# Graph attention over edge lists: extra columns in half-wide products, two-bank sums, and a later reciprocal

## The chip, the core and the metric

The kernel runs on one core of one Trainium2 chip. Times are device microseconds of a whole execution; the median of several runs is compared. The engines are TensorE (PE in the profile, its weight loads PEld), VectorE (DVE), ScalarE (ACT), GpSimd (POOL) and the queue that starts plain transfers (SP). TensorE writes its products into PSUM, the accumulator memory; the other data live in SBUF, the working memory, or in the main memory (DRAM).

## What is computed

Three graph attention layers over one graph of 4096 nodes, with features of width 512. The reference, cut to its core (`k` and `h` run over heads, `n` and `m` over nodes):

```python
# layer 0: 8 heads of 64, then a residual and a layer norm
h   = einsum('nf,kfp->knp', x, W)
f1  = einsum('knp,kp->kn', h, a_src); f2 = einsum('knp,kp->kn', h, a_dst)
e   = leaky_relu(f2[:, :, None] + f1[:, None, :], 0.2)
att = softmax(where(adj > 0, e, -1e16), axis=-1)
x   = layernorm(x + concat_heads(einsum('knm,kmp->knp', att, h)))
# layer 1: 8 heads of 64 (W1, a1), elu; then one head of 512 (Wo, ao), elu; then two dense layers
x1  = elu(concat_heads(gat_heads(x, adj, W1, a1)))
out = elu(gat_heads(x1, adj, Wo, ao))
out = relu(out @ lin1_w + lin1_b) @ lin2_w + lin2_b
x   = layernorm(x + out)
```

Everything is float32. The graph is sparse (on average 8 neighbours) with degrees that fall from the first node to the last: node `i` is joined to node `j` with a probability that is proportional to `1 / sqrt((i+1)(j+1))`.

## The kernel before

Nodes are taken in 32 tiles of 128. A first stage turns each tile's rows of the adjacency into lists of edges: `idx` holds the neighbour of each edge, `nl` the node that it belongs to, in chunks of 128 edges, separately for the two halves of 64 nodes of a tile. A tile of low degree has 6 chunks, the densest has 55, and a layer has 339. Beside it, each tile of `x` is projected. (A dense version of everything stands ready for graphs that don't fit the lists; it doesn't run here.)

A layer's input is a table in DRAM with one row per node: 512 projected features and, for each head, `d`, the part of the score that depends on the neighbour. The part that depends on the node itself, `s`, stays in SBUF. Both are products of the node's features with the weights' sums `wa` (the projection weights times the attention vector):

```python
def project_in(sb, ps, st, src, t, tag="pa"):
    pt = ps.tile([P, FC, P], F32, name="pt")
    for c in range(FC):                                   # FC = 4 blocks of 128 features
        nc.tensor.transpose(pt[:, c, :], src[:, ts(c, P)], ident)
    xt = sb.tile([P, FC, P], F32, name="xt")
    for c in range(FC):
        nc.scalar.activation(xt[:, c, :], pt[:, c, :], AF.Copy, accum_out=st.xparts[:, c, t : t + 1])
    ph = ps.tile([P, hs, dm], F32, name="ph")             # 512 columns: the features
    for c in range(FC):
        nc.tensor.matmul(ph, xt[:, c, :], st.w[:, c], start=(c == 0), stop=(c == FC - 1))
    pa = ps.tile([P, 2, hs], F32, name="pa", tag=tag)     # 16 or 2 columns: s and d
    for c in range(FC):
        nc.tensor.matmul(pa, xt[:, c, :], st.wa[:, c], start=(c == 0), stop=(c == FC - 1))
    return ph, pa

def project_out(sb, st, ph, pa, t, n=P):
    hrow = ...
    nc.scalar.copy(hrow[:, :F], ph[:n].rearrange("p h d -> p (h d)"))
    nc.scalar.copy(hrow[:, F:], pa[:n, 1, :])
    nc.sync.dma_start(st.table[t * P : t * P + n, :], hrow)
    if t < NT:
        nc.scalar.copy(st.s[:, t, :], pa[:, 0, :])
```

A tile's chunks are worked in units of up to 6. `gather` fetches, for each chunk, the 128 neighbours' rows of the table by one indirect transfer that GpSimd issues, into one of five buffers `g`. `spread` brings `s` of a tile's nodes to its edges by small products (`pss`), summed up by VectorE (`collect`). `weights` computes the exponent of each edge and head, `add` sums:

```python
def weights(self, u):
    nc.vector.tensor_add(zz, u.pick(self.s[u.t], base), d)            # d: columns 512 and on of g
    nc.vector.scalar_tensor_tensor(z, z, ALPHA, z, op0=OP.mult, op1=OP.max)
    nc.vector.tensor_sub(zz, zz, u.pick(self.ls[u.t], base))
    u.w = self.wk.tile([P, GC, hs], F32, name="w")
    nc.scalar.activation(u.w[:, : u.n], z, AF.Exp)
    if hs > 1:
        u.wp = self.ps.tile([P, GC, hs], F32, name="wp")              # the same in PSUM
        nc.scalar.activation(u.wp[:, : u.n], z, AF.Exp)

def add(self, u):
    if u.first:
        self.acc[u.t] = self.pacc.tile([P, F], F32, name="acc")       # two buffers
        self.den[u.t] = self.pacc.tile([P, hs], F32, name="den", bufs=1)
    # sm[edge, node] is 1 where the edge belongs to the node
    ...
    sums(self.den[u.t], (lambda k: u.w[:, k]) if hs > 1 else (lambda k: ones))
    if hs > 1:
        body = u.g[:, :n, :F].rearrange("p n (h w) -> p n h w", h=hs)
        nc.vector.tensor_mul(body, body, u.wp[:, :n, :, None].to_broadcast([P, n, hs, DM]))
    sums(self.acc[u.t], lambda k: u.g[:, k, :F])
```

`sums` makes one product per chunk, `sm` being the stationary side, into the 64 partitions of its half. The loop of a heads layer, each tile's normalization, transposition, projection and row store being spread over the steps that follow:

```python
def divide(t):                                  # o = acc * rd, residual, statistics (or the elu)
    o = at.normal(sb, t)
    return norm, t, o, finish(o, t, extra.pop(t))
def norm(t, o, rest):
    rest()                                      # the end of the layer norm (or of the elu)
    return project, t, o
def project(t, o):
    return rows, t, *project_in(pp, ps, nxt, o, t)
def rows(t, ph, pa):
    project_out(pp, nxt, ph, pa, t)
    if t % 8 == 0:
        split_s(pp, nxt, t, 8)

for i, u in enumerate(units):
    ...
    if u.first and pos + 2 < NT:
        spread = at.spread(order[pos + 2])
    run(project)
    if i + 1 < len(units):
        at.weights(units[i + 1])
    at.add(u)
    if i + GB < len(units):
        at.gather(units[i + GB])
    if u.last:
        at.inverse(sb, u.t)                     # rd = 1 / den
    run(rows)
    run(norm)
    if u.first and pos > 0:
        ways.append((divide, order[pos - 1]))
        run(divide)
    if spread:
        spread()
```

The order of instructions on each engine is that of this text in the three attention stages; each engine works its own list in order. The third stage (one head of 512) has a loop of the same kind, with `inverse` at the same place and the two dense layers between its units.

Of the kernel before, what the change touches and what calls it, by code (L numbers as in the profile page):

```python
# [32 lines left out]
HC = HID // P  # L33
ALPHA = 0.2
# [498 lines left out]
def sparse_path(  # L533
# [56 lines left out]
    class Stage2:  # L590
        def __init__(self, name, heads, dim, dest_first):
            self.name, self.heads, self.dim, self.dest_first = name, heads, dim, dest_first
            self.row = F + heads
            self.table = dram.tile([N + 1, self.row], F32, name=f"table_{name}")
            self.s = const.tile([P, NT, heads], F32, name=f"ss_{name}")
            self.s3 = const.tile([P, NT, 2, 3, heads], BF16, name=f"s3_{name}")
            self.xparts = const.tile([P, FC, NT], F32, name=f"xparts_{name}")
# [7 lines left out]
    def load_projection(pool, st, w, a):  # L605

        hs, dm = st.heads, st.dim
        st.w = pool.tile([P, FC, hs, dm], F32, name=f"sw_{st.name}")
        for c in range(FC):
            nc.sync.dma_start(st.w[:, c], w[:, ts(c, P), :].rearrange("k f o -> f k o"))  # L610
        st.wa = pool.tile([P, FC, 2, hs], F32, name=f"swa_{st.name}")
        with tc.tile_pool(name=f"swload_{st.name}", bufs=2) as wp:
            for side in range(2):
                ab = wp.tile([P, hs, dm], F32, name="sab")
                nc.sync.dma_start(ab, a[:, ts(side, dm)].partition_broadcast(P))
                at = side if st.dest_first else 1 - side
                for c in range(FC):
                    prod = wp.tile([P, hs, dm], F32, name="sprod")
                    nc.gpsimd.tensor_mul(prod, st.w[:, c], ab)
                    nc.vector.tensor_reduce(st.wa[:, c, at, :], prod, AX.X, OP.add)  # L620

    def project_in(sb, ps, st, src, t, tag="pa"):

        hs, dm = st.heads, st.dim
        pt = ps.tile([P, FC, P], F32, name="pt")
# [7 lines left out]
        ph = ps.tile([P, hs, dm], F32, name="ph")  # L633
        for c in range(FC):
            nc.tensor.matmul(ph, xt[:, c, :], st.w[:, c], start=(c == 0), stop=(c == FC - 1))  # L635
        pa = ps.tile([P, 2, hs], F32, name="pa", tag=tag)
        for c in range(FC):
            nc.tensor.matmul(pa, xt[:, c, :], st.wa[:, c], start=(c == 0), stop=(c == FC - 1))  # L638
        return ph, pa

    def project_out(sb, st, ph, pa, t, n=P):

        hrow = sb.tile([P, F + HS], F32, name="hrow")[:n, : st.row]
        nc.scalar.copy(hrow[:, :F], ph[:n].rearrange("p h d -> p (h d)"))  # L644
        nc.scalar.copy(hrow[:, F:], pa[:n, 1, :])
        nc.sync.dma_start(st.table[t * P : t * P + n, :], hrow)
        if t < NT:
            nc.scalar.copy(st.s[:, t, :], pa[:, 0, :])
# [17 lines left out]
    def project_mean(sb, ps, st, tag="pa"):  # L666

        hs, dm = st.heads, st.dim
# [3 lines left out]
        ph = ps.tile([P, hs, dm], F32, name="ph")  # L672
        for c in range(FC):
            nc.tensor.matmul(ph[:1], mean[:, c : c + 1], st.w[:, c], start=(c == 0), stop=(c == FC - 1))
        pa = ps.tile([P, 2, hs], F32, name="pa", tag=tag)
        for c in range(FC):
            nc.tensor.matmul(pa[:1], mean[:, c : c + 1], st.wa[:, c], start=(c == 0), stop=(c == FC - 1))
        project_out(sb, st, ph, pa, NT, 1)
# [224 lines left out]
    class Attention:  # L903
# [64 lines left out]
        def weights(self, u):  # L968
# [3 lines left out]
            zz = z.rearrange("p (m g) h -> p m g h", g=u.hn)  # L972
            d = u.g[:, : u.n, F : self.st.row].rearrange("p (m g) h -> p m g h", g=u.hn)
            nc.vector.tensor_add(zz, u.pick(self.s[u.t], base), d)  # L974
            nc.vector.scalar_tensor_tensor(z, z, ALPHA, z, op0=OP.mult, op1=OP.max)
            nc.vector.tensor_sub(zz, zz, u.pick(self.ls[u.t], base))
            u.w = self.wk.tile([P, GC, hs], F32, name="w")
            nc.scalar.activation(u.w[:, : u.n], z, AF.Exp)  # L978
            if hs > 1:

                u.wp = self.ps.tile([P, GC, hs], F32, name="wp")
                nc.scalar.activation(u.wp[:, : u.n], z, AF.Exp)  # L982

        def add(self, u):

            hs, n = self.st.heads, u.n
            if u.first:
                self.acc[u.t] = self.pacc.tile([P, F], F32, name="acc")
                self.den[u.t] = self.pacc.tile([P, hs], F32, name="den", bufs=1)
# [25 lines left out]
            def sums(out_, rows):  # L1015
                for k, (first, stop) in enumerate(flags):
                    h = k % u.hn
                    nc.tensor.matmul(out_[h * HN : (h + 1) * HN], sm[:, k], rows(k), start=first, stop=stop)  # L1018

            sums(self.den[u.t], (lambda k: u.w[:, k]) if hs > 1 else (lambda k: ones))  # L1020
            if hs > 1:
                body = u.g[:, :n, :F].rearrange("p n (h w) -> p n h w", h=hs)
                nc.vector.tensor_mul(body, body, u.wp[:, :n, :, None].to_broadcast([P, n, hs, DM]))  # L1023
            sums(self.acc[u.t], lambda k: u.g[:, k, :F])

        def inverse(self, sb, t):
            self.den[t], den = sb.tile([P, self.st.heads], F32, name="rd"), self.den[t]
            nc.vector.reciprocal(self.den[t], den)  # L1028

        def normal(self, sb, t):  # L1030
            o = sb.tile([P, F], F32, name="o")
            acc, rd = self.acc.pop(t), self.den.pop(t)
            if self.st.heads > 1:
                nc.vector.tensor_tensor(
                    o.rearrange("p (h w) -> p h w", w=DM),
                    acc.rearrange("p (h w) -> p h w", w=DM),
                    rd[:, :, None].to_broadcast([P, HS, DM]),
# [329 lines left out]
```

## Time and profile before

| | |
|---|---|
| median of 3 runs | 2692.4 us (2692.3 to 2696.59) |
| profiled execution | 2661.6 us, mean TensorE clock granted 0.846 |
| TensorE products / weight loads busy | 1993.7 us (75%) / 873.6 us (33%) |
| VectorE busy | 1507.3 us (57%) |
| ScalarE busy | 669.1 us (25%) |
| GpSimd busy | 1096.1 us (41%) |
| first gather of the three attention stages | 690, 1280 and 1861 us |

How to read the profile: a group is one line of the kernel on one engine, with the tiles written and read, the shape and the count; after the bar come its busy time, the mean ns of one instruction, and how long the engine was idle just before such instructions and what it waited for. "issue" is idle time in which nothing that the profile shows was waited for, and "remote" a releaser that it doesn't know. Line 1018 is the product inside `sums`, 635 and 638 are the two products of `project_in`, 644, 645 and 648 the copies of `project_out`, 914 is the gather, 1023 VectorE's multiply in `add`, 1028 the reciprocal, 1034 the normalization, 940 and 949 the products and the sum of `spread`. In a table of stretches each engine has its busy us and, in brackets, its instructions; PEclk is the granted share of TensorE's full clock. In a timeline a row has the start, the duration of the merged instructions, engine, line, operation, tiles, shape and count.

### The profile page before, as it was taken

What the parts mean: (1) busy time and instruction counts of PE and PEld (TensorE: products, weight loads), DVE (VectorE), ACT (ScalarE), POOL (GpSimd) and SP (SyncE); (2) the same over time, 40 slices, a digit from 0 to 9 for tenths busy, and PEclk for the clock granted to TensorE, in tenths of its full rate; (3) what the DMA queues carried; (4) which work ended last, traced back from release to release, by engine and by line L of the source; (5) the groups of instructions that cost most, each with busy time, mean ns of one, the idle gap of its engine ahead of it and who ended that gap; (6) DMA issues with size and microseconds to landing.
All of it is one profiled execution on the core that took longest, in us unless ns stands there. A gap on an engine that the chain in (4) does not pass through costs nothing. (4 is left out here: it accounts for less than half of the span.)

```text
span 2661.6 us, 27663 instructions
## 1 busy us (share of the span) xinstructions
PE 1993.7 (75%) x8501; PEld 873.6 (33%) x8501; DVE 1507.3 (57%) x4485; ACT 669.1 (25%) x1870; POOL 1096.1 (41%) x1204
## 2 busy tenths in 40 slices
PE   1125779999468787757488777666497999999998
PEld 0002234344134333323144333322243444444433
DVE  4998777788367777755356666553223233333331
ACT  1001233444045433221133222110121223322221
POOL 6100000000455666663646666553646544444310
PEclk9556678899689988877699888778697999999999
DMA  6101345564467877763556667564546444455421
GB/s 177 40 32 48 115 150 191 206 222 150 140 187 214 238 232 229 208 194 105 161 164 180 186 182 196 163 175 154 166 141 176 144 143 149 137 144 151 139 72 37
DMA packets 138069, 415.19 MB, mean 156 GB/s; under 512 B 33515, under 2 KB 33523, under 8 KB 133814
## 3 DMA queue, kind: packets, MB, share of 16 engines
q0 software_dynamic: 81360, 269.62, 36.2%
q1 hardware_dynamic: 56550, 143.70, 15.5%
q8 instruction: 70, 1.15, 0.2%
q14 instruction: 89, 0.73, 0.1%
HBM read 371.00 MB, written 42.23 MB: 155 GB/s over the span
## 5 line engine op out<-in xcount | busy, mean ns | idle before, releaser
L914 POOL DMA_INDIRECT g<-table_t,idx x1017 | 1029.4, 1012 | 846.4 <-PE acc L1018 305.3
L1018 PE MATMUL acc<-g,sm 128*64 128x512 f32 x2034 | 611.1, 682 | 80.6 <-issue 45.8
L635 PE MATMUL ph<-sw_t,xt 128*128 128x512 f32 x768 | 426.8, 698 | 97.9 <-issue 57.3
L1023 DVE TENSOR_TENSOR g<-g,wp 128x2048 f32<-128x2048 f32 (+4 forms) x148 | 383.4, 2591 | 33.1 <-ACT wp L982 23.0
L1018 PEld LDWEIGHTS acc<-g,sm 128*64 128x64 f32 x2034 | 169.8, 152 | 314.7 <-issue 270.5
L635 PEld LDWEIGHTS ph<-sw_t,xt 128*128 128x128 f32 x768 | 157.2, 220 | 282.2 <-issue 206.2
L1028 DVE RECIPROCAL rd<-den 128x8 f32<-128x8 f32 (+1 forms) x96 | 18.7, 194 | 388.1 <-PE den L1018 158.4
L765 POOL COPY over<-lst 128x1 f32<-128x1 f32 x35 | 6.6, 189 | 553.1 <-DVE lst L760 500.4
L1262 PE MATMUL p<-sl2w,shid 128*128 128x512 f32 x512 | 229.2, 600 | 3.3 <-DVE xr L1267 2.7
L1250 PE MATMUL p<-sht,sl1w 128*128 128x512 f32 x512 | 225.5, 596 | 0.0
L745 DVE MAX8 cand<-key 128x8 f32<-128x353 f32 (+55 forms) x467 | 204.9, 448 | 24.0 <-PE key L739 23.5
L729 ACT ACTIVATE sg<-raw 128x4096 bf16<-128x4096 int32 x32 | 116.0, 3625 | 217.7 <-PE key L738 208.8
L630 ACT ACTIVATE xt<-pt 128x128 f32<-128x128 f32 x384 | 101.1, 282 | 272.9 <-PE pt L627 127.3
L738 PE MATMUL key<-sg,s_identb 128*128 128x512 bf16 (+1 forms) x258 | 115.1, 446 | 48.2 <-DVE cand L745 28.0
L1262 PEld LDWEIGHTS p<-sl2w,shid 128*128 128x128 f32 x512 | 95.1, 191 | 137.4 <-issue 119.8
L1250 PEld LDWEIGHTS p<-sht,sl1w 128*128 128x128 f32 x512 | 95.5, 190 | 129.8 <-issue 124.9
L1018 PE MATMUL den<-w,sm 128*64 128x8 f32 x1356 | 71.8, 209 | 84.7 <-issue 38.3
L974 DVE TENSOR_TENSOR z<-s,g 128x48 f32<-128x48 f32 (+6 forms) x222 | 40.9, 184 | 150.7 <-DMA g<-table_t,idx 131.5
L644 ACT COPY hrow<-ph 128x512 f32<-128x512 f32 (+1 forms) x99 | 57.9, 585 | 271.6 <-PE ph L635 193.1
L1005 DVE TENSOR_SCALAR sm<-iota_n,nl,w 128x64 f32<-128x64 f32 x339 | 83.8, 325 | 71.1 <-ACT w L978 71.1
L638 PEld LDWEIGHTS pa<-swa_t,xt 128*128 128x128 f32 x768 | 106.8, 206 | 39.6 <-issue 24.2
L739 PE MATMUL key<-frac,ones_b 64*128 64x512 bf16 (+1 forms) x258 | 115.3, 447 | 0.0
(131 smaller groups left out, 2185.1 us busy)
## 6 DMA issues: line engine op xcount, KB each, us to landing
raw<-in_adj_dram SPq DMA_DIRECT2D x32, 2048.0 KB
table_t<-hrow SPq DMA_DIRECT2D x64, 260.0 KB
xr<-in_x_dram SPq DMA_DIRECT2D x64, 256.0 KB
g<-table_t,idx POOLq DMA_INDIRECT x1017
table_t<-hrow SPq DMA_DIRECT2D x32, 256.5 KB
sx_d<-o SPq DMA_DIRECT2D x32, 256.0 KB
xr<-sx_d SPq DMA_DIRECT2D x32, 256.0 KB
out_dram<-xr SPq DMA_DIRECT2D x32, 256.0 KB
```

Of the source, the lines that this page charges most:

```text
L630: nc.scalar.activation(xt[:, c, :], pt[:, c, :], AF.Copy, accum_out=st.xparts[:, c, t : t + 1])
L635: nc.tensor.matmul(ph, xt[:, c, :], st.w[:, c], start=(c == 0), stop=(c == FC - 1))
L638: nc.tensor.matmul(pa, xt[:, c, :], st.wa[:, c], start=(c == 0), stop=(c == FC - 1))
L729: nc.scalar.activation(sg, raw, AF.Sign)
L738: nc.tensor.matmul(key[:, j - w0_ : e - w0_], ident_b, sg[:, j:e], start=True, stop=False)
L739: nc.tensor.matmul(key[:, j - w0_ : e - w0_], ones_b, frac[:, j:e], start=False, stop=True)
L745: nc.vector.max(out=cand[:, at : at + 8], in_=part)
L914: nc.gpsimd.indirect_dma_start(out=u.g[:, k, : self.st.row], out_offset=None, in_=self.st.table[:, :], in_offset=bass.IndirectOffsetOnAxis ...
L1018: nc.tensor.matmul(out_[h * HN : (h + 1) * HN], sm[:, k], rows(k), start=first, stop=stop)
L1023: nc.vector.tensor_mul(body, body, u.wp[:, :n, :, None].to_broadcast([P, n, hs, DM]))
L1250: nc.tensor.matmul(p1, l1w[:, c, ts(k, P)], hts[b][:, c, :], start=(c == 0), stop=(c == FC - 1))
L1262: nc.tensor.matmul(p2, hids[b][:, k, ts(j, P)], l2w[:, k, :], start=(k == 0), stop=(k == HC - 1))
```

## The change

`s`, `d` and the softmax's denominators cease to be products of their own. The weights' sums are stored beside the projection weights, so that a projection is two products per block of 128 features, each of half the features (256) and 8 further columns (4 of `d`, 4 of `s`; with one head, one further column). A row of the table is now, twice over, 256 features and 4 `d`. In `weights` the exponent is written over the `d` columns of the gathered rows, and the sums take each half of a row with its 4 weights, 260 columns, into one of two PSUM banks; the denominators come out as columns of `acc`. `acc` now has two banks and two buffers, `den` is left to the one-head layer alone, and transposes and both halves of a projection share one pair of PSUM buffers. The reciprocal moves into the next unit's step, the transposes to the end of a step (the products that need them stay at the beginning of the following step), and `split_s` to the step after the rows. The purpose is to have fewer small products and fewer waits between TensorE and VectorE. The diff, cut (the loading of weights, shapes and stage 1's calls are left out):

```diff
-        pt = ps.tile([P, FC, P], F32, name="pt")
+    def turn_in(sb, ps, st, src, t):
+        pt = ps.tile([P, FC, P], F32, name="pt", tag="ph")
         (transposes and copies to xt as before)
-        ph = ps.tile([P, hs, dm], F32, name="ph")
-        for c in range(FC):
-            nc.tensor.matmul(ph, xt[:, c, :], st.w[:, c], start=(c == 0), stop=(c == FC - 1))
-        pa = ps.tile([P, 2, hs], F32, name="pa", tag=tag)
-        for c in range(FC):
-            nc.tensor.matmul(pa, xt[:, c, :], st.wa[:, c], start=(c == 0), stop=(c == FC - 1))
-        return ph, pa
+    def project_in(ps, st, columns, n=P):
+        halves = []
+        for j in range(2):
+            ph = ps.tile([P, st.wide], F32, name="ph")
+            for c in range(FC):
+                nc.tensor.matmul(ph[:n], columns(c), st.w[:, c, j], start=(c == 0), stop=(c == FC - 1))
+            halves.append(ph)
+        return halves
 ...
-        nc.scalar.copy(hrow[:, :F], ph[:n].rearrange("p h d -> p (h d)"))
-        nc.scalar.copy(hrow[:, F:], pa[:n, 1, :])
+        for j, ph in enumerate(halves):
+            part = HF + hs // 2 if hs > 1 else HF + j
+            nc.scalar.copy(hrow[:, j * st.part : j * st.part + part], ph[:n, :part])
         nc.sync.dma_start(st.table[t * P : t * P + n, :], hrow)
         if t < NT:
-            nc.scalar.copy(st.s[:, t, :], pa[:, 0, :])
+            for j, ph in enumerate(halves):
+                m = hs // 2 if hs > 1 else 1 - j
+                if m:
+                    nc.scalar.copy(st.s[:, t, j * m : (j + 1) * m], ph[:, st.wide - m :])
 ...
             if hs > 1:
+                nc.scalar.activation(d, zd, AF.Exp)          # d: the columns in the gathered rows
                 u.wp = self.ps.tile([P, GC, hs], F32, name="wp")
                 nc.scalar.activation(u.wp[:, : u.n], z, AF.Exp)
 ...
-                self.acc[u.t] = self.pacc.tile([P, F], F32, name="acc")
-                self.den[u.t] = self.pacc.tile([P, hs], F32, name="den", bufs=1)
+                self.acc[u.t] = self.pacc.tile([P, 2, F], F32, name="acc")     # heads > 1
 ...
-            sums(self.den[u.t], (lambda k: u.w[:, k]) if hs > 1 else (lambda k: ones))
-            if hs > 1:
-                (multiply)
-            sums(self.acc[u.t], lambda k: u.g[:, k, :F])
+            if hs > 1:
+                (multiply, on the 256 feature columns of each half)
+                for m in range(u.pairs):
+                    for j in range(2):
+                        sums(self.acc[u.t][:, j, :part], lambda k: halves[:, 2 * k + j],
+                             range(m * u.hn, (m + 1) * u.hn))
+            else:
+                sums(self.den[u.t], lambda k: ones)
+                sums(self.acc[u.t], lambda k: u.g[:, k, :F])
 ...
             def divide(t):
+                at.inverse(sb, t)
                 o = at.normal(sb, t)
                 return norm, t, o, finish(o, t, extra.pop(t))
             def norm(t, o, rest):
                 rest()
-                return project, t, o
-            def project(t, o):
-                return rows, t, *project_in(pp, ps, nxt, o, t)
+                xt = turn_in(pp, ps, nxt, o, t)
+                return project, t, xt
+            def project(t, xt):
+                return rows, t, project_in(ps, nxt, lambda c: xt[:, c, :])
 ...
-                if u.last:
-                    at.inverse(sb, u.t)
+                run(split)
                 run(rows)
                 run(norm)
 ...
     (the one-head layer)
+            if u.first and pos > 0:
+                at.inverse(sb, order[pos - 1])
             at.add(u)
             if i + GT < len(units):
                 at.gather(units[i + GT])
-            if u.last:
-                at.inverse(sb, u.t)
```

## The prediction

> **What bounds the kernel now.** I read the page first (engines, groups), then the busy time by stretches, then the waits of VectorE (DVE), then the timeline of single tiles. The run has three parts: the edge finding with the first projection (0 to 690 us), two layers of eight heads (690 to 1280 and 1280 to 1861 us), and the one-head layer with the dense pair (1861 to 2662 us). The change touches mostly the two layers. From the page, the groups it rewrites (line, engine, operation, count, then busy us and mean ns of one, then idle time ahead of them):
>
> ```profile
> L914 POOL DMA_INDIRECT g<-table_t,idx x1017 | 1029.4, 1012 | 846.4 <-PE acc L1018 305.3
> L1018 PE MATMUL acc<-g,sm 128*64 128x512 f32 x2034 | 611.1, 682 | 80.6 <-issue 45.8
> L635 PE MATMUL ph<-sw_t,xt 128*128 128x512 f32 x768 | 426.8, 698 | 97.9 <-issue 57.3
> L1028 DVE RECIPROCAL rd<-den 128x8 f32<-128x8 f32 (+1 forms) x96 | 18.7, 194 | 388.1 <-PE den L1018 158.4
> L1018 PE MATMUL den<-w,sm 128*64 128x8 f32 x1356 | 71.8, 209 | 84.7 <-issue 38.3
> L638 PEld LDWEIGHTS pa<-swa_t,xt 128*128 128x128 f32 x768 | 106.8, 206 | 39.6 <-issue 24.2
> ```
>
> The 96 reciprocals do 18.7 us of work, but VectorE stands idle 388.1 us just before them. The two layers hold 64 of them and 256.8 us of that idle time (the groups kept apart by shape). Next, what four stretches of the layers look like:
>
> ```profile
> core 0: us, PE busy (x) PEld busy (x) DVE busy (x) ACT busy (x) POOL busy (x), PEclk, DMA share, GB/s
> 690.00:755.00 65.00, 20.88 (x86) 6.89 (x87) 24.78 (x42) 6.83 (x19) 47.19 (x48) 0.55 0.73 208
> 755.00:855.00 100.00, 86.42 (x470) 42.32 (x470) 73.13 (x148) 50.98 (x162) 43.62 (x44) 0.97 0.63 190
> 855.00:1180.00 325.00, 249.31 (x1380) 113.55 (x1382) 235.66 (x430) 111.65 (x376) 215.47 (x213) 0.90 0.75 222
> 1680.00:1861.00 181.00, 116.05 (x568) 48.97 (x564) 86.12 (x137) 23.16 (x109) 89.01 (x89) 0.78 0.56 163
> ```
>
> No engine is full. GpSimd issues a gather of 1.00 us every 1.30 us when it runs freely (timeline at 690 us), so 339 gathers per layer need at least 339 x 1.30 = 441 us; the layers take 590 and 581 us from first gather to the next layer's first gather. Some 35 us of each are the drain after the last gather. So about 115 and 105 us per layer are lost to coupling. The timeline of one tile in the stretch of light tiles (first TensorE, then VectorE) shows how:
>
> ```profile
> 795.22 0.27 PE L940 MATMUL pss<-s_t,s 128*128 128x48 bf16 x4 [0.76 <-DVE s L949]
> 795.34 0.63 PE L627 MATMUL pt<-s_ident,o 128*128 128x128 f32 x4
> 796.43 3.70 PE L635 MATMUL ph<-sw_t,xt 128*128 128x512 f32 x8 [0.46 <-issue]
> 799.97 0.96 PE L638 MATMUL pa<-swa_t,xt 128*128 128x16 f32 x8
> 800.86 0.52 PE L1018 MATMUL den<-w,sm 128*64 128x8 f32 x12
> 801.23 2.77 PE L1018 MATMUL acc<-g,sm 128*64 128x512 f32 x12
> ```
>
> ```profile
> 796.59 3.34 DVE L1023 TENSOR_TENSOR g<-g,wp 128x3072 f32<-128x3072 f32 x1
> 801.43 0.21 DVE L1028 RECIPROCAL rd<-den 128x8 f32<-128x8 f32 x1 [1.50 <-PE den L1018]
> 802.16 0.69 DVE L1034 TENSOR_TENSOR o<-acc,rd 128x512 f32<-128x512 f32 x1
> 804.44 0.32 DVE L949 TENSOR_REDUCE s<-pss 128x64 f32<-128x192 f32 x1
> ```
>
> This is a loop between two in-order engines. VectorE's reciprocal waits for the tile's last `den`; that comes behind the scores, transposes, `ph` and `pa` on TensorE; the next tile's scores wait in turn for VectorE's `collect` (804.44), which comes behind the reciprocal. One turn is 9.59 us (from this reciprocal to the next at 811.02), of which VectorE works some 8.2 and TensorE, by the starts above, some 8.3.
>
> **What the Trainium skill says.** (1) "TensorE: Matmul & The Clock Gate", section "Back-to-back issue gap": a stream of products costs time in proportion to its columns plus a few ns. The trace agrees in the form and differs in the size for float32: each product is two PE instructions here, and 16 of 512 columns take 7.06 us (the chain at 1969 us), 0.441 us each, where the page has 0.216. I use 0.441. (2) The same page, section "Step-by-step: what each phase is for": weight loads are pulled ahead of running products. The trace agrees: the loads of L635 (0.19 us) start every 0.43 us while the products run on without a gap. (3) The same page, section "What's actually happening": the array's clock falls to half in idle and recovers under load. The trace agrees (0.55 and 0.97 in the first two stretches above). (4) "PSUM — Partial Sum Buffer", section "Specifications (TRN2)": eight banks of 512 float32. This is why 512 + 8 columns are cut in two halves; no run here shows the limit itself. By the diff the layer pools fill eight banks both before (2 acc, 1 den, 2 small, 3 projection) and after (4 acc, 2 small, 2 projection).
>
> **Projection.** Before: 8 instructions of 512 columns, 3.54 us (796.43 to 799.97), then 8 of 16 or 2 columns that are little but their weight loads, 0.89 us (799.97 to 800.86): 4.43 us. After: 16 instructions of 264 or 257 columns. Estimate by columns: 0.441 x 264/512 = 0.227 us, above the 0.11 us pace at which `pa` shows loads can follow each other, so the loads stay hidden: 16 x 0.227 = 3.64 us. Saved 0.8 us per tile at full clock. ScalarE has two copies of some 0.3 us for one of 0.585, and one more tiny copy (0.17): +0.25 us, beside other work.
>
> **Sums.** Two node halves run together: the loads of `acc` start in twos every 0.43 us, 0.215 us for each of 12 instructions (2.6 us for 6 chunks). `den` adds 12 at 0.045 us. After, each chunk has 2 x 2 instructions of 260 columns, estimate 0.215 x 260/512 = 0.109: 24 x 0.109 = 2.62 us. So `acc` stays as it is and `den` goes: 0.37 us (800.86 to 801.23) per six chunks, 0.06 per chunk. What `den` did in the shadow of VectorE's multiply (2.3 to 3.35 us) can no longer be done there, but the sums' own work is not longer. The exponent now also goes into the gathered tile; the count of ScalarE instructions is unchanged.
>
> **Transposes and the two loops.** Before, TensorE transposed and waited for ScalarE's copy (0.46 us above; 97.9 us idle ahead of L635 in all). After, the next step's scores lie between. That hides perhaps half, 0.25 us per tile. TensorE's work thus drops by 0.8 + 0.37 = 1.2 us in a light tile, to about 7.1, and its wait for the copy by 0.25. The reciprocal moves behind the next unit's multiply, where its sums are long finished, and `den`'s single buffer, which made the next tile's first `den` wait for it, is gone. The loop above is then open: VectorE's own 8.2 us (0.7 weights, 0.55 `sm`, 3.35 multiply, 3.1 normalization, 0.6 collect) is the longest, so I expect about 8.7 instead of 9.59.
>
> **The sum, by tiles.** Spacing of reciprocals before, against 1.30 us per gather:
> - 9 tiles of 6 chunks: 9.6 (layer 0) and 8.7 us (layer 1) where steady, floor 7.8; the first ones lose up to 22 us to cold clock and stalls. Estimate 8.7 and 8.1, and a little back of the cold ones: -12 and -9 us.
> - 10 tiles of 8: on average 12.5 and 13.2 us, floor 10.4; estimate 11.0 and 11.7: -15 each.
> - the tile of 7 and that of 11, which have a last unit of one chunk whose multiply gives almost no cover: 17 to 18 and 24 us, floors 9.1 and 14.3; -8 for both.
> - 10 to 12 chunks: already at 14.6 to 16 for floors 13.0 and 15.6: -2.
> - 14 to 55 chunks: 187 and 194 us, floor 160; a third to a half of the excess: -12 and -14.
>
> That is -49 and -48; I take 95 for both. In the edge finding, TensorE is full only from 400 to 675 us (24 of 25 us): 21 tiles of 12.5 us there, 0.8 us at a clock of 0.87 each, less what VectorE (20 of 25) leaves: -12. Before 400 us VectorE bounds it: 0. In the last layer TensorE is busy 693 of 762 us in its main part with nothing removed; the later reciprocal lets `sm` start earlier (33 us of `den` waiting for `sm` there): -5. Sum: 95 + 12 + 5 = 112, so 2692 - 112 = 2580 us.
>
> **Rivals.** *The wait only moves.* The reciprocal's 257 us become the same wait at the normalization one step later, or GpSimd's 1.30 us rhythm takes over at once. For it: GpSimd's 213 gathers x 1.30 = 277 of 325 us in the third stretch. Against it: TensorE waits for VectorE and VectorE for TensorE in the same turn, which is a loop and not a bound. Then only TensorE's shorter work counts: about 2645. *Half-wide products don't pay.* If a load of 0.19 us were not hidden behind 0.227 us, a projection would cost 16 x 0.33 = 5.3 us, 0.9 more than before, and the sums would grow as well. Against it: the 0.11 us pace of `pa`. It would make the layers about 60 us and the edge finding 20 us longer: some 2750 with part of the loop's gain back. *The shared pair of projection banks* (transposes and both halves in turn) makes TensorE wait for ScalarE's copies. In the layers the copies come a sum earlier; in the edge finding ScalarE's 3.6 us sign conversion can stand ahead of them: +10 to +20 us, some 2595. *More is gained*: if the layers come near their gather floor everywhere, 2 x 80 us: 2510.
>
> **Range and chances.** The gain of the layers is the uncertain term (50 to 160); 2530 to 2650 holds the first and most of the last rival. Faster by over 2% means under 2638.6: 0.78. Within 2%: 0.16. Slower needs exposed loads: 0.06.
>
> **What would show it.** Right: idle ahead of the reciprocal in the layers falls from 257 to under 80 us; turns of light tiles at 8.5 to 8.9 us in layer 0; half-wide products at 0.22 to 0.24 us in a row in projections and 0.11 in sums; GpSimd's busy share in the layers rises from 687 of 1171 to about 687 of 1075. Wrong: product spacing above 0.3 us, or idle of like size at the normalization (`o<-acc,rd`), or ScalarE copies ahead of transposes. A lower clock in the layers than the 0.85 to 0.88 of now would also take the gain away.

## The result and the profile after

The changed kernel takes 2576.57 us (median of 4 runs, 2571.56 to 2583.41) against 2692.35 us (4 runs, 2687.74 to 2696.59) beside it: a ratio of 0.9572, 95% interval 0.9545 to 0.9599. The forecast was 2580. The sum was right; its terms were not. From first gather to first gather, profile against profile (in us):

| stage | before | after | measured | forecast |
|---|---|---|---|---|
| edge finding and first projection | 689.7 | 641.1 | -48.6 | -12 |
| two layers of heads | 585.1 + 587.0 | 566.9 + 562.5 | -42.7 | -95 |
| one-head layer and dense pair | 799.8 | 805.0 | +5.2 | -5 |

(The profiled execution of the kernel before, 2661.6 us, lies some 1.1% under its median, so these differences add to 86 us and not to 116. The 30 us between can't be placed in a stage. The second layer's first gather comes at 1274.8 us in the profile before, and not at 1280 as stated ahead of the prediction and in it; so the layers took 585.1 and 587.0 us, not 590 and 581.)

The costliest groups of the page after that answer to those shown of before: the gather and the projection's products.

```profile
L938 POOL DMA_INDIRECT g<-table_t,idx x1017 | 1030.1, 1013 | 806.6 <-PE acc L1057 305.1
L663 PE MATMUL ph<-sw_t,xt 128*128 128x264 f32 (+1 forms) x1536 | 410.5, 422 | 90.4 <-ACT xt L652 60.2
```

With the shapes kept apart, the layers' reciprocal before, and the heads' sums and the layers' reciprocal after:

```profile
L1028 DVE RECIPROCAL rd<-den 128x8 f32<-128x8 f32 x64 | 13.3, 207 | 256.8 <-PE acc L1018 82.0 <-PE den L1018 77.0 <-remote 48.1
L1057 PE MATMUL acc<-g,sm 128*64 128x260 f32 x2712 | 417.7, 437 | 251.4 <-DVE g L1065 110.8 <-issue 88.2 <-DMA g<-table_t,idx 51.6
L1081 DVE RECIPROCAL rd<-acc 128x8 f32<-128x8 f32 x64 | 12.8, 201 | 38.7 <-remote 23.3 <-PE acc L1057 15.4
```

The 64 reciprocals of the layers now have 38.7 us of idle time ahead of them instead of 256.8, and the `den` products of the heads are gone. That part of the forecast came true, and yet the layers gained less than half of it. The waits of VectorE in the two layers say where the idle time went (engine, line, what was waited for; us in all, times, longest; the largest, and those that the text reads). Before:

```profile
DVE z L974 <- DMA g<-table_t,idx: 90.8, 17, 12.4
DVE rd L1028 <- PE acc L1018: 82.0, 19, 13.7
DVE rd L1028 <- PE den L1018: 77.0, 23, 13.9
DVE rd L1028 <- remote: 48.1, 7, 10.7
DVE o L1049 <- ACT ex L1048: 8.0, 3, 3.5
```

After:

```profile
DVE z L1003 <- DMA g<-table_t,idx: 122.2, 24, 16.9
DVE o L1108 <- ACT ex L1107: 38.8, 12, 5.2
DVE rstd L1119 <- ACT rstd L1116: 37.4, 16, 4.8
```

VectorE now waits for the landing of the next gather (`z`), for the elu's exponential (`ex`) and for the layer norm's root (`rstd`). All waits of each kind added, the idle time ahead of the reciprocal fell by 218 us, and 173 us came back at three other places: 100 ahead of the ends of the elu and the layer norm, most of it waiting for ScalarE (from 16 to 116 us), 44 ahead of `collect` (L949, now L973: from 21 to 66) and 29 ahead of `z` (from 100 to 129). On this chip, then, the largest part moved to results of ScalarE and not to the gathers. VectorE's work in the layers is unchanged (696.9 us of 1171 before, 704.5 of 1129 after), and so is GpSimd's (687.3, 685.3).

The edge finding has changed in another way. Stretches of the kernel before (us; busy us and instructions of PE, PEld, DVE, ACT, POOL; granted clock, DMA share, GB/s; the last line of each set is the whole time to 640 us):

```profile
0.00:210.00 210.00, 40.96 (x89) 12.35 (x90) 168.92 (x681) 15.26 (x22) 56.39 (x124) 0.68 0.26 79
400.00:640.00 240.00, 230.98 (x804) 98.77 (x803) 191.75 (x825) 101.88 (x230) 6.16 (x38) 0.87 0.59 208
0.00:640.00 640.00, 405.96 (x1268) 165.19 (x1268) 512.02 (x2158) 160.95 (x348) 65.56 (x180) 0.75 0.40 137
```

The same of the changed kernel:

```profile
0.00:210.00 210.00, 133.44 (x586) 101.10 (x589) 163.19 (x664) 65.49 (x324) 55.29 (x124) 0.98 0.43 141
280.00:400.00 120.00, 78.42 (x192) 21.49 (x194) 109.11 (x479) 28.42 (x8) 2.42 (x15) 0.50 0.34 123
400.00:640.00 240.00, 199.19 (x476) 53.77 (x483) 209.75 (x921) 69.97 (x22) 6.93 (x43) 0.51 0.43 158
0.00:640.00 640.00, 455.97 (x1417) 200.63 (x1434) 545.38 (x2331) 182.01 (x419) 65.52 (x187) 0.69 0.40 139
```

586 TensorE instructions stand in the first 210 us instead of 89, and 476 instead of 804 from 400 to 640 us: the projections of most tiles have moved from the stretch where TensorE was full to the one where it was idle. No line of the diff as cut shows this. In the instruction list the tiles' transposes stood, before, behind 0, 3, 5, 22, 22, 30, 46 and so on of the edge finding's 258 `frac` products (L739, now L763), spread all through it; after, nearly all stand behind the first 5 to 22.

### The profile page after: what moved, and what is told of

Its sections match the earlier page's. It is cut to its first block, busy times and chain, and to the rows that moved or that the text cites. A ratio compares the mean times of both kernels' runs of the same rounds, so it can differ in the third digit from the quotient of the medians.

```text
span 2575.5 us, 28031 instructions
## 1 busy us (share of the span) xinstructions
PE 1919.6 (75%) x8484; PEld 1001.2 (39%) x8501; DVE 1510.6 (59%) x4485; ACT 671.6 (26%) x1934; POOL 1095.6 (43%) x1204
## 4 chain that ended last, share of the span: by engine, by line
PE 29%; issue 14%; DVE 8%; POOL 8%; DMA 5%; another core or an unknown queue 5%; ACT 3%; POOLq 1%; DVEq 0%; ACTq 0%
PE acc L1057 9%; PE p L1315 8%; POOL g L938 8%; PE p L1327 5%; PE ph L663 5%; DMA g<-table_t,idx 5%; DVE g L1065 3%; PE den L1057 1%; PE pt L649 1%; POOLq L938 1%; DVE sm L1035 1%; ACT L1116 0%; PE pss L964 0%; DVE sm L1044 0%
## 5 line engine op out<-in xcount | busy, mean ns | idle before, releaser
L1057 PE MATMUL acc<-g,sm 128*64 128x260 f32 (+1 forms) x3390 | 618.5, 485 | 251.4 <-DVE g L1065 110.8
L1057 PEld LDWEIGHTS acc<-g,sm 128*64 128x64 f32 x3390 | 290.4, 154 | 494.2 <-issue 289.0
L663 PE MATMUL ph<-sw_t,xt 128*128 128x264 f32 (+1 forms) x1536 | 410.5, 422 | 90.4 <-ACT xt L652 60.2
L663 PEld LDWEIGHTS ph<-sw_t,xt 128*128 128x128 f32 x1536 | 310.8, 208 | 164.4 <-ACT xt L652 73.5
L673 ACT COPY hrow<-ph 128x260 f32<-128x260 f32 (+3 forms) x198 | 72.5, 375 | 425.3 <-PE ph L663 246.9
L762 PE MATMUL key<-sg,s_identb 128*128 128x512 bf16 (+1 forms) x241 | 142.4, 591 | 42.6 <-DVE cand L769 20.9
L763 PE MATMUL key<-frac,ones_b 64*128 64x512 bf16 (+1 forms) x258 | 151.4, 587 | 6.7 <-issue 5.3
L1108 DVE SCALAR_TENSOR_TENSOR o<-ex,o 128x512 f32<-128x512 f32 x64 | 44.4, 693 | 172.0 <-ACT ex L1107 128.3
L1318 ACT ACTIVATE shid<-p,sl1b 128x512 f32<-128x512 f32 x64 | 44.0, 687 | 231.9 <-PE p L1315 192.4
L973 DVE TENSOR_REDUCE s<-pss 128x48 f32<-128x144 f32 (+13 forms) x108 | 35.0, 324 | 94.0 <-remote 44.7
```

The source lines that it names most:

```text
L663: nc.tensor.matmul(ph[:n], columns(c), st.w[:, c, j], start=(c == 0), stop=(c == FC - 1))
L762: nc.tensor.matmul(key[:, j - w0_ : e - w0_], ident_b, sg[:, j:e], start=True, stop=False)
L763: nc.tensor.matmul(key[:, j - w0_ : e - w0_], ones_b, frac[:, j:e], start=False, stop=True)
```

## The experiments

Two theories for the edge finding: **the banks** (before, the projection's narrow product `pa` shared the PSUM buffers `small` with the edge finding's own small products, which ties the order of the two; the changed kernel has an own pair of buffers for the projection), and **the half-wide products** (less TensorE work in the full stretch). For the layers: **the reciprocal's wait was the loss**, as the prediction has it; against it **the wait only moves**, that VectorE's idle time lies where it would wait for a gather anyhow; and ScalarE's order and the gather buffers as what limits now. The letters of the theories are each expectation's own. The first four kernels ran on one chip (before beside them: 2686.68 us, 7 runs), which is called the first chip together with that of the result (2692.35 us), the other eight on a second chip, on which the kernel before takes 2497.78 (15 runs, with the first four of the eight) and 2500.13 us (21 runs, with the last four). Times are compared within a chip, by the ratio to before. The diffs show the lines that matter; signatures, tags and calls for the last tile that follow from them are left out. One of the eight runs of "after, reciprocal early" on the second chip had a granted clock of 0.687 and took 2772.91 us; it is not in its ratio.

| kernel | median us | ratio to before, interval | stages (us) |
|---|---|---|---|
| first chip: before, own pair of banks | 2634.12 | 0.9802, 0.9761 to 0.9842 | 646.9, 599.8, 577.5, 807.2 |
| after, shared banks | 2580.60 | 0.9595, 0.9556 to 0.9634 | 652.5, 571.8, 564.0, 798.3 |
| after, reciprocal early | 2634.27 | 0.9802, 0.9744 to 0.9860 | 640.4, 614.4, 573.0, 799.6 |
| after, transposes late | 2572.47 | 0.9580, 0.9537 to 0.9624 | 641.9, 569.9, 563.7, 795.1 |
| second chip: after again | 2416.00 | 0.9658, 0.9640 to 0.9676 | 641.9, 501.8, 492.1, 778.5 |
| after, reciprocal early | 2514.00 | 1.0044, 1.0024 to 1.0064 | 642.6, 580.2, 513.0, 776.6 |
| before, reciprocal late | 2492.22 | 0.9977, 0.9962 to 0.9991 | 692.1, 512.8, 504.6, 784.3 |
| the same, again | 2495.02 | 0.9985, 0.9971 to 0.9999 | 690.0, 519.6, 505.8, 785.2 |
| after, full-width products | 2429.66 | 0.9730, 0.9699 to 0.9761 | 648.1, 503.7, 499.5, 776.0 |
| after, divide ahead of the rows | 2409.75 | 0.9654, 0.9638 to 0.9670 | 641.1, 501.8, 492.0, 781.4 |
| after, six gather buffers | 2402.29 | 0.9622, 0.9606 to 0.9639 | 641.8, 494.9, 489.1, 776.6 |
| after, divide ahead and seven buffers | 2390.77 | 0.9553, 0.9532 to 0.9575 | 640.6, 488.4, 481.5, 778.6 |

### The kernel before, its first projection in an own pair of banks

```diff
+        pq = pools.enter_context(tc.tile_pool(name="eq", bufs=2, space=PSUM))
-            project_out(sb, st0, *project_in(sb, ps, st0, xr, t, "small"), t)
+            project_out(sb, st0, *project_in(sb, pq, st0, xr, t, "one", "one", "one"), t)
```

(`pt`, `ph` and `pa` all take turns in that one pair; nothing else differs from before.)

> The kernel before, with one part of the change alone: in the edge finding, transposes, wide product and narrow product of a projection rotate through one pair of PSUM buffers of their own, instead of three single banks of which the narrow product shares one with the edge finding's own small product. Theory A (the bank that was shared tied each projection to its tile's edge finding): the projections run ahead, the first gather starts near 642 us instead of 690, and the time falls by 40 to 50 us to some 2645. Rival B (the half-wide products' smaller TensorE work is what shortened the edge finding): the first gather stays within 8 us of 690 and the time within 10 us of before.

The first gather comes at 646.9 us instead of 689.7: 43 us, with full-width products and a separate `pa`. The stretches look like those of the changed kernel:

```profile
0.00:210.00 210.00, 140.11 (x542) 76.54 (x545) 160.19 (x645) 60.05 (x276) 55.91 (x124) 0.99 0.44 136
400.00:640.00 240.00, 199.41 (x459) 52.99 (x468) 211.72 (x921) 72.34 (x20) 6.89 (x43) 0.50 0.43 158
```

542 TensorE instructions in the first 210 us: the buffers alone move the projections forward. The time falls by 53 us, of which the stages ascribe 43 to this one; the other 10 aren't placed. Nothing in the layers was changed. The edit does two things at once: the projection leaves the bank that it shared with the edge finding's small product, and it gets two buffers in turn where it had three single ones. Which of the two matters was not separated.

### The changed kernel, its first projection in the shared banks

```diff
-            xt = turn_in(sb, pp, st0, xr, t)
-            project_out(sb, st0, project_in(pp, st0, lambda c: xt[:, c, :]), t)
+            xt = turn_in(sb, ps, st0, xr, t, "pt")
+            project_out(sb, st0, project_in(ps, st0, lambda c: xt[:, c, :], tags=("ph", "small")), t)
```

> The changed kernel with only the edge finding's PSUM put back: transposes and first half in single banks, the second half in the bank of the edge finding's small product. Theory A: the first gather moves back from 641 to 680 to 695 us, the time rises by 40 to 50 us to some 2622. Rival B: the first gather stays within 8 us of 641 and the time at 2577.

If the banks were all of the gain, the first gather should have gone back to some 690 us. It comes at 652.5, only 11 us later than in the changed kernel. The order is that of before again (88 instructions in the first stretch), and still most of the gain is there:

```profile
0.00:210.00 210.00, 36.36 (x88) 12.48 (x90) 169.49 (x683) 15.07 (x24) 55.02 (x124) 0.68 0.24 79
400.00:640.00 240.00, 218.03 (x893) 116.30 (x908) 217.15 (x944) 110.66 (x276) 7.17 (x45) 0.97 0.56 207
```

Against before in the same stretch TensorE is busy for 218 us instead of 231 and has 893 instructions instead of 804 behind it, at a clock of 0.97 instead of 0.87, and VectorE gets through 217 us of work instead of 192. So each cause gains nearly all of it without the other (43 and 37 us), and both together 49. The cap that they share looks to be VectorE: it does 543 to 545 us of work before 640 us in all three kernels, and did 512 in the kernel before. What this kernel keeps of the change in this stage is the half-wide products with the copies and the loading of weights that belong to them; these were not taken apart. What lets the clock rise here (the shorter products, or their number) isn't separated.

### The changed kernel, the layers' reciprocal where it was

```diff
             def divide(t):
-                at.inverse(sb, t)
                 o = at.normal(sb, t)
 ...
+                if u.last:
+                    at.inverse(sb, u.t)
                 run(split)
```

> The changed kernel with the reciprocal of the two heads layers back at the end of a tile's last unit; all else as changed. Theory A (the later reciprocal opened the loop and is what the layers gained): idle ahead of the reciprocal is back over 200 us in the layers, both layers take at least their 585 us of before, the time is 2615 or more. Rival B (the layers gained because the small products went away): idle moves about but the time stays within 10 us of 2577.

On the first chip: 2634.27 instead of 2576.57 us, 58 us back. The waits of VectorE from 640 to 1828 us:

```profile
DVE rd L1081 <- PE acc L1057: 169.0, 44, 6.2
DVE z L1003 <- DMA g<-table_t,idx: 90.8, 17, 17.3
DVE rd L1081 <- remote: 89.9, 11, 18.6
DVE rd L1081 <- issue: 40.4, 8, 8.9
```

299 us of idle time stand ahead of the reciprocal. It looks like proof of the prediction. The counterpart, the kernel before with only this moved, says otherwise on the second chip (below). The same kernel on the second chip:

> As e3 (the changed kernel with the heads layers' reciprocal back at the end of a tile's last unit), now beside the changed kernel on the same chip. Theory A (the late reciprocal is worth what e3 showed wherever it runs): 50 to 60 us slower than the changed kernel. Theory A' (its worth depends on late completions of TensorE's products, which the quicker chip shows few of): on a quicker chip 10 to 30 us slower, on a slower one 50 to 60. Rival B: within 8 us.

There it costs 98 us against the changed kernel, more than any of the theories had it, and makes the whole slower than before, though the edge finding keeps its 48 us. Its waits of VectorE in the layers, and then those of the changed kernel on that chip:

```profile
DVE rd L1081 <- PE acc L1057: 249.4, 64, 9.5
DVE z L1003 <- DMA g<-table_t,idx: 96.5, 24, 17.3
```

```profile
DVE z L1003 <- DMA g<-table_t,idx: 192.4, 65, 17.1
DVE s L973 <- PE pss L964: 28.5, 9, 8.0
DVE s L685 <- ACT ss_t L679: 14.0, 2, 7.3
DVE rd L1081 <- PE acc L1057: 13.4, 5, 6.6
```

All 64 reciprocals wait, and all for `acc`: with the denominators as columns of the sum there is no early result, and VectorE stops until the whole sum is done. Against the changed kernel there are 236 us more of such idle time, of which 96 come back as shorter waits for the gather; the layers grow by 99.

### The kernel before, only the reciprocal moved

```diff
+                if u.first and pos > 0:
+                    at.inverse(sb, order[pos - 1])
                 at.add(u)
 ...
-                if u.last:
-                    at.inverse(sb, u.t)
```

> The kernel before with the reciprocal of the heads layers alone moved: from the end of a tile's last unit to ahead of the next unit's sums; products, banks and buffers as before. Theory A (the move by itself opens the loop): 40 to 60 us faster than before, some 2635; idle ahead of the reciprocal under 100 us in the layers. Rival B (the small products of the denominators, still behind the projection on TensorE and with one buffer, keep the wait): less than 20 us faster. The first gather stays at 690 in both.

> As e8 (the kernel before with the reciprocal alone moved). Theory A' (the chip made e8 and e3 differ): on a slower chip 40 to 60 us faster than before, on a quicker one some 6 as in e8. Theory D (the separate denominators with one buffer made them differ, since the next tile's sums then wait for the reciprocal): under 20 us faster than before on either chip, and less than r2 loses.

The ratios are 0.9977 and 0.9985, so about 5 us, twice. In the second of them the wait is gone as planned, and the largest now is the gather's landing:

```profile
DVE z L974 <- DMA g<-table_t,idx: 172.5, 64, 12.6
DVE s L654 <- ACT ss_t L648: 53.2, 8, 10.1
DVE s L949 <- PE pss L940: 28.6, 9, 7.2
DVE rd L1028 <- PE den L1018: 18.1, 7, 4.8
```

On this chip this tells the two theories of the layers apart: taking away the wait on which the prediction put most of its 95 us gives 5. That VectorE would have waited for its gather there anyway is what these waits suggest; how long the reciprocal waited on this chip in the kernel before was not profiled. A rival can be set aside: with one `den` buffer the next tile's first `den` could have to wait for the moved reciprocal, so that the loop stays closed. No wait of TensorE in these layers ends with the reciprocal; where `den` waits, it is for `sm`, which VectorE makes after it:

```profile
PE den L1018 <- DVE sm L996: 79.5, 26, 21.7
```

On the first chip this kernel was not run, so whether the move alone gains more there stays open.

### Transposes late

```diff
-                xt = turn_in(pp, ps, nxt, o, t)
-                return project, t, xt
-            def project(t, xt):
+                return project, t, o
+            def project(t, o):
+                xt = turn_in(pp, ps, nxt, o, t)
```

> The changed kernel with the transposes of the heads layers back at the beginning of the following step, ahead of their products; all else as changed. Theory A (the transposes' place hides only part of a wait of 0.46 us per tile): 5 to 15 us slower, 2582 to 2592. Rival B (the earlier transposes start the next projection sooner and so shorten a loop through ScalarE's copies): more than 25 us slower. Rival C: they cost nothing or help nowhere: within 4 us of 2577.

0.9580 (0.9537 to 0.9624) against 0.9572 (0.9545 to 0.9599): moving the transposes to the end of a step is worth nothing that shows, and the stages differ by 1 to 3 us in the layers.

### Full-width products

```diff
-        for j in range(2):
-            ph = ps.tile([P, st.wide], F32, name="ph")
+        for w, wide in ((st.wf, F), (st.wa.rearrange("p c s h -> p c (s h)"), 2 * st.heads)):
+            ph = ps.tile([P, wide], F32, name="ph", tag="ph")
             for c in range(FC):
-                nc.tensor.matmul(ph[:n], columns(c), st.w[:, c, j], start=(c == 0), stop=(c == FC - 1))
+                nc.tensor.matmul(ph[:n], columns(c), w[:, c], start=(c == 0), stop=(c == FC - 1))
```

(The table's layout, the sums and the banks stay those of the changed kernel; `s` and `d` are copied out of a product of their own again.)

> The changed kernel with the projection's products as before: per block of 128 features one of 512 columns and one of 16 or 2, copied into the new row layout; sums, reciprocal, buffers and order stay changed. Theory A (a projection's smaller TensorE work, 0.8 us, is on the path of most tiles): 25 to 50 us slower, mostly in the two layers. Rival B (after the reciprocal's move TensorE has slack there): within 8 us of 2577. The first gather stays near 641 us in both.

2429.66 against 2416.00 us on the second chip: the half-wide products are worth 14 us by the medians, 18 by the ratios. The stages give 6 us of it in the edge finding and 2 and 7 in the layers.

### What limits the layers now

```diff
                 run(split)
+                early = divide(order[pos - 1]) if u.first and pos > 0 else None
                 run(rows)
                 run(norm)
-                if u.first and pos > 0:
-                    ways.append((divide, order[pos - 1]))
-                    run(divide)
+                if early:
+                    ways.append(early)
```

(The normalization's root then stands ahead of the row copies on ScalarE.)

> The changed kernel with one order altered in the heads layers: the previous tile's normalization (with its root or its two exponentials on ScalarE) is issued ahead of the row copies of the tile before it. Theory A (what holds the changed layers is a loop: projection, then on ScalarE the row copies that wait for it, then the root, then VectorE's end of the norm, the transposes, the next projection): tiles of 8 chunks go from 12.0 us to 11 or less, the time falls by 15 to 35 us to some 2550. Rival B (the loop has slack, gathers or late completions hold the tiles): within 6 us of 2577, or slower because the rows now wait for the root.

> The changed kernel itself, unaltered, so that the runs beside it have a reference on their own chip: the chip of the last four runs took 2498 us for the kernel before where the first chip took 2687. If this chip is of the quicker kind: about 0.966 of before (edge finding 49 us, layers some 35 us); if of the slower kind: 0.957 as measured.

0.9654 (0.9638 to 0.9670) against 0.9658 (0.9640 to 0.9676) for the changed kernel itself: no gain on the second chip, so ScalarE's order doesn't limit it there. In the layers of the changed kernel on this chip VectorE waits 5.6 us for `ex` and 2.6 us for `rstd`, where the first chip has 38.8 and 37.4; on the first chip this order was not run, nor were more gather buffers. The repetition of the changed kernel is the yardstick for all eight, and it shows what the second chip lacks, late copies. One tile of 8 chunks on the first chip (start, duration, engine, line):

```profile
801.17 3.83 PE L663 MATMUL ph<-sw_t,xt 128*128 128x264 f32 x16 [0.36 <-ACT wp L1010]
...
808.77 0.65 ACT L673 COPY hrow<-ph 128x260 f32<-128x260 f32 x2 [5.42 <-remote]
...
810.87 0.29 ACT L1116 ACTIVATE rstd<-mv,s_eps 128x1 f32<-128x1 f32 x1
...
811.19 0.16 DVE L1119 RECIPROCAL rstd<-rstd 128x1 f32<-128x1 f32 x1 [1.94 <-issue]
```

On the second:

```profile
801.18 3.83 PE L663 MATMUL ph<-sw_t,xt 128*128 128x264 f32 x16 [0.36 <-ACT xt L652]
...
803.27 0.38 ACT L673 COPY hrow<-ph 128x260 f32<-128x260 f32 x1 [1.15 <-PE ph L663]
...
805.05 0.38 ACT L673 COPY hrow<-ph 128x260 f32<-128x260 f32 x1 [1.40 <-PE ph L663]
...
806.87 0.29 ACT L1116 ACTIVATE rstd<-mv,s_eps 128x1 f32<-128x1 f32 x1
...
807.91 0.16 DVE L1119 RECIPROCAL rstd<-rstd 128x1 f32<-128x1 f32 x1
```

The 16 products run alike, to a hundredth. On the second chip each copy follows its half at once; on the first both halves are copied some 4 us after the last product, for a releaser that the profile doesn't know, and the root and VectorE come 4.0 and 3.3 us later. The half-wide products' pace was in the forecast, the late copy was not.

```diff
-GB = 5
+GB = 6
```

> The changed kernel with six instead of five gather buffers in the heads layers. Theory A (the layers are now held by gathers that wait for a free buffer: GpSimd waits 97 us for TensorE's sums and VectorE 122 us for landings): 15 to 30 us faster, some 2555. Rival B (these waits are slack behind another loop): within 6 us of 2577.

0.9622 (0.9606 to 0.9639) against 0.9658: one more buffer `g` gives about 9 us by the ratios and 14 by the medians, 7 and 3 us of it in the layers by the stages. VectorE's waits for the landing of gathers from 641 to 1770 us fall from 225.9 to 196.8 us. Both edits together, with seven buffers:

> The changed kernel with e5's order and seven gather buffers. If both edits work on waits of their own: 10 to 30 us faster than the changed kernel on a quicker chip, 30 to 60 on a slower one, with the layers within 40 us of their gathers' 441 us plus the 35 us drain. If e5's order does nothing by itself, it equals e9: 5 to 15 us faster.

2390.77 us (2382.85 to 2393.5), ratio 0.9553 (0.9532 to 0.9575): 25 us under the changed kernel on the same chip. The layers take 488.4 and 481.5 us, 12.4 and 5.5 above the 476 us that the gathers' rhythm (441) and the drain (35) allow. Which of the two edits brings what beyond the sixth buffer's gain was not run.

## Why the prediction was right, and where it wasn't

The total came out right because one term was 37 us too small and another some 50 us too large; the rest lies in the 30 us that no stage can be given. That it came so near is luck.

- **Edge finding, forecast -12, measured -48.6.** The step failed: it charged only "0.8 us at a clock of 0.87" per tile in the full stretch. It took "Before 400 us VectorE bounds it" as a reason for a gain of zero there, when it is the reason why TensorE has room there. The own pair of banks moves the projections into that room (-43 by itself), and the shorter products relieve the full stretch by more than their own 0.8 us, with a higher clock (-37 by themselves). The two don't add; VectorE's 545 us of work seem to be what comes next.
- **Layers, forecast -95, measured -43** (-48 against the kernel with the own pair of banks, whose layers are those of before and whose profiled execution lies at its median). The premise failed, that the time above the gather floor was a loop that the reciprocal closes. On the first chip 218 us of idle time ahead of it went, and the layers gained 43 by the whole change. On the second the reciprocal alone gives 5 us in the kernel before. "The wait only moves" was the nearer rival, though not "at the normalization" (`o<-acc,rd`), which waits for nothing now: on the first chip most of the wait moved to the ends of the elu and the layer norm (16 to 116 us), and VectorE's waits for the landing of gathers rose from 91 to 122 us only. What the late copies on ScalarE have to do with that is suggested by the tile shown above, not shown. On the second chip the layers of the kernel with only the reciprocal moved take some 150 us less than those of before on the first (1172); so most of the 220 us that the prediction called "lost to coupling" is missing there, where the move itself gives only 5. In figures, these layers take 1017 and 1025 us, and those of the changed kernel 994: 23 to 31 us for the rest of the change, of which the half-wide products are some 9. What is left (14 to 22) would be the `den` products' and the two-bank sums'; no run shows that part by itself.
- **"But the sums' own work is not longer"** was right (the sums of all three layers and the heads' `den` took 611.1 + 71.8 us before and 618.5 after) and missed the cost of giving up the shadow: without `den` the early reciprocal would stop VectorE at every tile (+99 us in the layers of the second chip, +58 in all on the first). The late reciprocal is what makes the denominators' columns bearable. It is a repair of the change's other half, not the source of the gain.
- **Half-wide products** went as worked out: 16 in 3.83 us (forecast 3.64), with the loads hidden; the rival of exposed loads falls.
- **Transposes at the end of a step**, forecast 0.25 us per tile: nothing.
- **Shared pair of banks**, feared at +10 to +20 in the edge finding, is the largest single gain there.
- **One-head layer, forecast -5.** The pair of profiles shows +5.2, but the same code spreads: with the changed loop 795.1 to 805.0 on the first chip, with the old one 799.8 and 807.2. On the second chip the six profiles with the changed loop give 776.0 to 781.4 and the two with the old 784.3 and 785.2, some 7 us apart. That fits the forecast; the reciprocal was not moved there by itself, so its cause is only argued.
- **Signs**: idle time ahead of the reciprocal under 80 us (38.7), and projection products every 0.22 us, as forecast. The granted clock in the layers, 0.84, is that of before. Four turns of light tiles in layer 0 that took 9.5 to 9.6 us each before take 7.9 to 9.4 (forecast 8.5 to 8.9), and tiles of 8 chunks 12.3 and 11.6 us on average (12.5 and 13.2 before, forecast 11.0 and 11.7). But "GpSimd's busy share" came to 685 of 1129 us and not of 1075, which is the missing half of the layers' gain.

## What to carry to other kernels

Idle time in front of an instruction is not time lost: before counting it, ask what the engine would wait for next if that wait were gone, and test the move by itself in the kernel before. When a result becomes part of a larger sum, its first reader has to wait for all of it, so move that reader in the same step. An own pair of PSUM buffers can let a chain of products run where its engine is idle (43 us here), even if nothing of its work is saved.

## What was unexpected of the hardware

Two chips differ by 7% with the same kernel: 2686.68 and 2497.78 us for the one before. The edge finding is alike on both (689.7 us on the first; 690.0 and 692.1 with the late reciprocal on the second), so the difference lies in the layers and the one-head layer. From 641 to 1900 us the waits of all engines for an unknown releaser add up to 162 us (before) and 305 us (after) on the first chip, and to none in any profile of the second. In the kernel before, on the first chip, at 721 us, eight products of a sum run together and then four one at a time:

```profile
721.50 3.76 PE L1018 MATMUL acc<-g,sm 128*64 128x512 f32 x8 [2.65 <-DVE g L1023]
726.36 1.01 PE L1018 MATMUL acc<-g,sm 128*64 128x512 f32 x1 [1.10 <-issue]
727.75 1.01 PE L1018 MATMUL acc<-g,sm 128*64 128x512 f32 x1 [0.38 <-issue]
729.84 1.01 PE L1018 MATMUL acc<-g,sm 128*64 128x512 f32 x1 [1.08 <-issue]
```

The same sum on the second chip, in the kernel before with the late reciprocal:

```profile
722.35 5.38 PE L1018 MATMUL acc<-g,sm 128*64 128x512 f32 x12 [2.65 <-DVE g L1023]
```

So on the first chip products, or the readers of products as in the tile shown above, lag at some times with nothing in the profile to hold them; why isn't settled.

The other surprise is the clock. With the projections gone from the stretch from 280 to 640 us, TensorE runs this stretch at 0.50 to 0.51 of its clock, though it is busy for 199 of the last 240 us. The edge finding is still 49 us shorter, and VectorE, busy for 210 of those 240 us, waits for TensorE for some 40 us from 280 to 640 us (74 in the kernel before, at 0.82 of the clock). What a higher clock would bring there no run shows.
